# A path that fetches the last tile of a group row by row on the SyncE queue, beside the GpSimd gathers of a graph network

## The chip, the cores and the metric

The kernel runs on one core of a Trainium2 chip. The metric is the device time of one execution in microseconds, as the median of a few runs; a profiled execution shows where the time lies. The core has five engines that work side by side, each with its own instruction queue: TensorE (PE, with its weight loads PEld), VectorE (DVE), ScalarE (ACT), GpSimd (POOL) and SyncE (SP), which only issues transfers. The transfers themselves are done by 16 DMA engines.

## The reference

The kernel computes one message-passing layer of a graph network with 12,500 nodes and 412,500 edges, sorted by receiver. Cut to what matters:

```
h   = relu(layernorm(x))                                  # 12500 x 64
msg = concat(h[src], h[dst], edge_attr)                   # 412500 x 160
m   = silu(msg @ W1 + b1) @ W2 + b2                       # 412500 x 64
a   = softmax(silu(msg @ Wa1 + ba1) @ Wa2 + ba2, axis=0)  # over all edges
agg = segment_sum(m * a, dst)                             # 12500 x 64
out = x + silu(concat(h, agg) @ Wu1 + bu1) @ Wu2 + bu2
```

## The kernel before

**Node stage.** The nodes are normalised and multiplied once by the sender part and once by the receiver part of the two first layers (W1 and Wa1 side by side, C = 128 columns). That gives two tables in memory with one row of 128 floats (512 bytes) for each node: `ts_d`, looked up by sender, and `tr_d`, looked up by receiver.

**Edge loop.** The edges are cut into tiles of P = 128, and K = 8 tiles make a group: 3224 tiles, NG = 403 groups. For each group `load(g)` does the following:

- GpSimd issues eight indirect gathers (L412), one for each tile. A gather takes 128 sender numbers from a column of `src_sb` and brings 128 rows of `ts_d` into `gs[:, j, :]`, one row for each partition. The pool `gather` has 8 buffers of one group each.
- Every fourth group, SP loads the edge features and the receiver numbers of four groups (`eo`, L421, and `db`, L424), and `registers` (L399) loads four window bases from `base_sb` into SP's registers.
- SP loads two windows of 32 rows of `tr_d` at the address in a register (L431) into one of three `wins` buffers. Since the edges are sorted, all receivers of a group lie near each other.
- DVE builds a one-hot matrix from the receivers (L435), and PE multiplies it, together with the edge features, with the window (L439). So `pe` holds the receiver part and the edge part for the 1024 edges.

`begin(g)` adds the gathered rows to it on DVE (L444) and takes tanh on ACT (L445). `end(g)` forms both silu results (L455, L461), the attention logit (L463, L466) and, every fourth group, a running maximum. `sum_up` weights the edges of an earlier group (L507), sums them by receiver on PE (L513), projects them (L524) and adds them into `sums` in on-chip memory (L534 to L538). A buffer of `gather` is free again when `end(g)` has read it, and the gather of group g + 8 then goes into it.

**Order.** `load` runs AHEAD = 2 groups before `begin`. The instructions of DVE, ACT and PE in the loop are held in program order by `pin`. The gathers and SP's transfers are not: a planner orders each queue when the program is built, with earlier program lines first among those that it takes to be ready. From group 16 to about group 112 the loop also carries, every second group, a piece of work on the nodes (`node_bias` and `node_rest`, the `hb` loads of L315 and L333 and the stores of L324 and L335 on SP).

**Node update.** After the loop each node's sum is scaled and run through the update layers, and the result is written out.

The lines around which all this turns:

```
for g in range(AHEAD):
    load(g)
...
for g in range(NG):
    ...
    begin(g)
    ...
    if g + AHEAD < NG:
        load(g + AHEAD)
    ...
    end(g)
```

Of the kernel before, what the change touches and what calls it, by code (L numbers as in the profile page):

```python
# [42 lines left out]
F32 = mybir.dt.float32  # L43
I32 = mybir.dt.int32
AF = mybir.ActivationFunctionType
ALU = mybir.AluOpType
AX = mybir.AxisListType
ENG = mybir.EngineType
# [3 lines left out]
P = 128  # L52
# [3 lines left out]
C = 2 * U  # L56
S1 = U + 1
K = 8
# [7 lines left out]
B = 4  # L66
NQ = 4
TABLES = 4
EPS = 1e-5
NEG = -3.0e38  # L70
BIG = 3.0e38
# [5 lines left out]
WHY = "a receiver's number; windows past the last node are padded"  # L77


@with_exitstack  # L80
def gnn_kernel(ctx: ExitStack, tc: tile.TileContext, n_edges, x, src, dst, dst_row, first, edge,
               weights, out):
    nc = tc.nc
    NB = x.shape[0] // P
    T = src.shape[1]
    NG = T // K
    NP = NB * P
# [6 lines left out]
    ts_d = dram.tile([NP, C], F32, name="ts_d")  # L94
# [12 lines left out]
    part, at = {}, 0  # L107
# [43 lines left out]
    with tc.tile_pool(name="node1", bufs=1) as node1, \  # L151
# [23 lines left out]
        pin = tc.keep_in_program_order  # L175
# [15 lines left out]
        eps = node1.tile([P, 1], F32, name="eps")  # L191
        nc.vector.memset(eps, EPS)
        pin(nc.scalar.activation(node1.tile([P, 1], F32, name="spare"), eps, AF.Sqrt))
# [90 lines left out]
        for c, nn in chunks:  # L284
            tr = node.tile([P, CB, C], F32, name="tr")[:, :nn, :]
            for b in range(0, nn, 4):
                n = min(4, nn - b)
                pn = node_ps.tile([P, 4, C], F32, name="pn", bufs=4)
                for i in range(0, n, 2):
# [7 lines left out]
        pin(nc.scalar.dma_start(hT_d, hT))  # L297

    one_pass(tc, n_edges, locals())
    again = nc.values_load(wrong[0:1, 0:1], min_val=0, max_val=1,  # L300
                           skip_runtime_bounds_check_because="it is the outcome of a comparison")
# [36 lines left out]
def one_pass(tc, n_edges, v):  # L338
    nc = tc.nc
    NB, T, NG, NP, CB = (v[k] for k in ("NB", "T", "NG", "NP", "CB"))  # L340
# [3 lines left out]
    ts_d, tr_d, bq_d, edge, dst_row = (v[k] for k in ("ts_d", "tr_d", "bq_d", "edge", "dst_row"))  # L344
# [8 lines left out]
    pin = tc.keep_in_program_order  # L353

    with ExitStack() as ctx:
# [16 lines left out]
        for w in wins:  # L372
            nc.vector.memset(w, 0.0)
            for r in range(2):
                rows = slice(WR + r * DE, WR + (r + 1) * DE)
                nc.vector.tensor_copy(w[rows, :, r, :], we[rows, None, :].to_broadcast([DE, 2, C]))
        with tc.tile_pool(name="work2", bufs=2) as work2, \
                tc.tile_pool(name="small", bufs=3) as small, \
                tc.tile_pool(name="pre_ps", bufs=AHEAD + 1, space=PSUM) as pre_ps, \
                tc.tile_pool(name="one_ps", bufs=1, space=PSUM) as one_ps:  # L380
            pes, gss, lgs, ps_, psums, sps, pps, ees, mts = ({} for _ in range(9))


            w2t_ps = one_ps.tile([P, 4, P], F32, name="mt")[:U, 0, :S1]
# [4 lines left out]
            nc.tensor.matmul(w2u_ps, w2t, wu1a, start=True, stop=True)  # L389
            nc.vector.tensor_copy(w2u, w2u_ps)  # L390
            at_sp, at_dve = {}, {}


            tr_w = bass.AP(tensor=tr_d.tensor, offset=tr_d.offset,
# [2 lines left out]
            def registers(g, engine, at):  # L397
                n = min(NQ, NG - g)
                _, regs = nc.values_load_multi_w_load_instructions(  # L399
                    base_sb[0:1, g:g + n], engines=[engine], min_val=0, max_val=NP - 1,  # L400
                    skip_runtime_bounds_check_because=WHY)
                for i in range(n):
                    at[g + i] = regs[i]

            def load(g):

                t = g * K
                if g % NQ == 0:
                    registers(g, ENG.SP, at_sp)
                gs = gss[g] = gather.tile([P, K, C], F32, name="gs")  # L410
                for j in range(K):
                    nc.gpsimd.indirect_dma_start(  # L412
                        out=gs[:, j, :], out_offset=None, in_=ts_d[:, :],
                        in_offset=bass.IndirectOffsetOnAxis(ap=src_sb[:, t + j:t + j + 1], axis=0))
                if g % NQ == 0:
                    n = min(NQ, NG - g) * E2
                    eo = work2.tile([P, NQ, E2], F32, name="eo")
                    db = work2.tile([WR, NQ, E2], I32, name="db")
                    for i in range(g, min(g + NQ, NG)):
                        ees[i] = eo[:, i - g, :], db[:, i - g, :]  # L420
                    nc.sync.dma_start(eo.rearrange("p g e -> p (g e)")[WR:, :n],  # L421
                                      edge[:, g * E2:g * E2 + n])
                    for r in range(2):
                        nc.sync.dma_start(  # L424
                            db.rearrange("p g e -> p (g e)")[r * R:(r + 1) * R, :n],
                            bass.AP(tensor=dst_row.tensor, offset=dst_row[r:r + 1, g * E2:].offset,
                                    ap=[[0, R], [1, n]]))
                eo, db = ees.pop(g)
                win = wins[g % WINS]
                for r in range(2):  # L430
                    nc.sync.dma_start(win[r * R:(r + 1) * R, :, r, :],  # L431
                                      tr_w[bass.ds(at_sp[g], R), :, :])
                for h in range(2):
                    e = slice(h * E2 // 2, (h + 1) * E2 // 2)
                    pin(nc.vector.tensor_scalar(eo[:WR, e], db[:, e], bj[:, g, h:h + 1], None,  # L435
                                                op0=ALU.is_equal))
                pe = pes[g] = pre_ps.tile([P, K, C], F32, name="pe")
                for q in range(H):
                    pin(nc.tensor.matmul(pe[:, 2 * q:2 * q + 2, :], eo[:, q * P:(q + 1) * P],  # L439
                                         win[:, q // 2, :, :], start=True, stop=True))  # L440

            def begin(g):

                pin(nc.vector.tensor_tensor(gss[g], pes[g], gss[g], ALU.add))  # L444
                pin(nc.scalar.activation(pes[g], gss[g], AF.Tanh))  # L445

            def end(g):
# [94 lines left out]
            at, weighed = [None, None], [0]  # L542
# [28 lines left out]
            for g in range(AHEAD):  # L571
                load(g)
            done = 0
            for g in range(NG):
# [3 lines left out]
                if more and g == NG - 1:  # L578
                    next(more)
                begin(g)  # L580
                if more and g < NG - 1:
                    next(more)
# [6 lines left out]
                if g + AHEAD < NG:  # L589
                    load(g + AHEAD)  # L590
# [36 lines left out]
        with tc.tile_pool(name="upd1", bufs=1) as upd1, \  # L627
# [14 lines left out]
            for c in range(0, NB, 2 * H):  # L642
                n = min(H, (NB - c) // 2)
# [32 lines left out]
def general(tc, n_edges, v, dst):  # L676
# [7 lines left out]
    with ExitStack() as ctx:  # L684
        keep = ctx.enter_context(tc.tile_pool(name="keep_g", bufs=1))
        act_d = dram.tile([P, T, S1], F32, name="act_d")
        sum_d = [dram.tile([NP + P, S1], F32, name=f"sum_d{r}") for r in range(TABLES)]
        before = keep.tile([P, P], F32, name="before")
# [15 lines left out]
        rows = (NP + P) // P  # L704
        for r in range(TABLES):
            flat = sum_d[r].rearrange("(p b) f -> p (b f)", p=P)
# [63 lines left out]
        with tc.tile_pool(name="sums_g", bufs=2) as work, \  # L770
                tc.tile_pool(name="sums_g_ps", bufs=2, space=PSUM) as sums_ps:
            for g in range(0, T, G):
# [3 lines left out]
                for k in range(0, ng, K):  # L776
# [26 lines left out]
                    for j in range(K):  # L803
                        nc.gpsimd.indirect_dma_start(
                            out=sum_d[(t + j) % TABLES][:, :],
                            out_offset=bass.IndirectOffsetOnAxis(ap=to[:, j:j + 1], axis=0),
# [6 lines left out]
        with tc.tile_pool(name="upd_g", bufs=2) as work, \  # L813
                tc.tile_pool(name="upd_g_ps", bufs=2, space=PSUM) as upd_ps:
            for c in range(0, NB, CB):
                part = work.tile([P, TABLES, CB, S1], F32, name="part")
                for r in range(TABLES):
                    nc.sync.dma_start(part[:, r], sum_v[r][:, c:c + CB, :])
                for r in range(1, TABLES):
                    nc.vector.tensor_tensor(part[:, 0], part[:, 0], part[:, r], ALU.add)  # L820
# [95 lines left out]
```

## Time and profile before

| | us |
|---|---|
| median of 3 runs | 4156.85 (4156.84 to 4158.81) |
| the profiled execution | 4156.93 |
| its span, first to last instruction | 4155.2 |
| POOL busy | 3048.2 (73%) |
| DVE busy | 2874.9 (69%) |
| PE busy / PE weight loads | 2243.6 (54%) / 1682.4 (40%) |
| ACT busy | 599.4 (14%) |
| first gather starts / last gather starts | 52.0 / 4082.0 |

Busy time counts the work of an engine. Loading registers, waiting on semaphores and issuing transfers on SP are not counted as busy; their durations can still be read by line, under the name "SPq". A group of the page reads: line, engine, operation, output and inputs, shapes, count, then busy us and mean ns of one, then the idle time in front of it and what ended that. "issue" means that nothing in the profile was being waited for.

### The profile page before, as it was taken

The page shows a single profiled execution, that of the slowest core. Times are in us where ns is not written, and L with a number is a line of the kernel's source. Part 1 is how long each engine was busy: PE and PEld are TensorE (multiplying, and loading weights), DVE is VectorE, ACT ScalarE, POOL GpSimd, SP SyncE. Part 2 cuts the span into 40 slices and gives each one's busy share as a digit, 9 for nine tenths or more (in the row PEclk, how much of TensorE's full clock was granted, in tenths as well). Part 3 has the DMA queues.
Part 4 walks back from the last instruction along what each step waited for, and adds up shares of the span by engine and source line. Part 5 has one row for each costly group of instructions (what it writes and reads, how often), then busy time and mean ns, then how long its engine had stood idle before and what let it go on. Part 6 is the DMA issues. An engine that isn't in the chain of part 4 may idle for free.

```text
span 4155.2 us, 43768 instructions
## 1 busy us (share of the span) xinstructions
PE 2243.6 (54%) x10980; PEld 1682.4 (40%) x10980; DVE 2874.9 (69%) x7698; ACT 599.4 (14%) x1230; POOL 3048.2 (73%) x3236
## 2 busy tenths in 40 slices
PE   5545555545465555555555555555555555555555
PEld 4433333433344344434443344434433443444444
DVE  6767776666677676666766666666676666766668
ACT  3211111111111111111111111111111111111112
POOL 3777777777777777777777777777777777777772
PEclk8666666676666665665566656566566556656565
DMA  7433443433433333333333333333333333333323
GB/s 275 109 87 94 102 101 95 103 96 99 102 85 90 90 80 90 86 83 90 81 90 85 85 90 80 90 85 85 90 80 90 85 85 90 80 90 85 86 77 111
DMA packets 230872, 392.46 MB, mean 94 GB/s; under 512 B 97746, under 2 KB 156371, under 8 KB 217427
## 3 DMA queue, kind: packets, MB, share of 16 engines
q0 software_dynamic: 103168, 211.49, 20.6%
q1 hardware_dynamic: 126066, 168.42, 15.6%
q10 hardware_dynamic: 1376, 9.67, 0.6%
q8 instruction: 91, 1.49, 0.1%
q14 instruction: 171, 1.39, 0.1%
HBM read 363.56 MB, written 25.72 MB: 94 GB/s over the span
## 4 chain that ended last, share of the span: by engine, by line


## 5 line engine op out<-in xcount | busy, mean ns | idle before, releaser
L412 POOL DMA_INDIRECT gs<-ts_d,src_sb x3224 | 3046.6, 945 | 1033.9 <-issue 933.7
L439 PE MATMUL pe<-wins,eo 128*128 128x256 f32 x3224 | 1401.8, 611 | 1187.4 <-issue 1124.1
L439 PEld LDWEIGHTS pe<-wins,eo 128*128 128x128 f32 x3224 | 958.4, 312 | 1464.9 <-issue 1191.1
L444 DVE TENSOR_TENSOR gs<-pe,gs 128x1024 f32<-128x1024 f32 x403 | 491.7, 1220 | 1107.0 <-DMA gs<-ts_d,src_sb 1088.1
L445 ACT ACTIVATE pe<-gs 128x1024 f32<-128x1024 f32 x403 | 415.7, 1031 | 2751.9 <-DVE gs L444 2058.6
L507 DVE TENSOR_SCALAR wt<-iota_w,dloc,p 128x40 f32<-128x40 f32 x3224 | 723.1, 317 | 0.1
L513 PE MATMUL sp<-wt,acts 128*65 128x40 f32 x6448 | 585.3, 261 | 0.9 <-DVE wt L507 0.9
L513 PEld LDWEIGHTS sp<-wt,acts 128*65 128x65 f32 x6448 | 534.6, 173 | 26.7 <-DVE wt L507 1.0
L483 PE MATMUL mt<-ident,mx 128*128 128x128 f32 x103 | 48.4, 470 | 506.9 <-DVE sums L537 503.6
L455 DVE SCALAR_TENSOR_TENSOR acts<-pe,gs 128x512 f32<-128x512 f32 x403 | 271.7, 674 | 29.7 <-ACT pe L445 29.6
L463 DVE TENSOR_TENSOR pe<-pe,w_all 128x512 f32<-128x512 f32 x403 | 281.5, 699 | 12.8
L461 DVE SCALAR_TENSOR_TENSOR pe<-pe,gs 128x512 f32<-128x512 f32 x403 | 280.6, 696 | 11.2
L466 DVE TENSOR_REDUCE lg<-pe 128x8 f32<-128x512 f32 x403 | 277.0, 687 | 10.3
L435 DVE TENSOR_SCALAR eo<-db,bj 64x256 f32<-64x256 int32 x806 | 273.1, 376 | 7.6
L524 PEld LDWEIGHTS mt<-ss,w2u 65*64 65x64 f32 x806 | 99.8, 176 | 397.2 <-issue 383.8
L524 PE MATMUL mt<-ss,w2u 65*64 65x40 f32 x806 | 150.6, 281 | 166.1 <-DVE gm L490 148.8
L483 PEld LDWEIGHTS mt<-ident,mx 128*128 128x128 f32 x103 | 18.6, 181 | 519.9 <-DVE sums L537 515.7
L494 ACT ACTIVATE scale<-fall 128x1 f32<-128x1 f32 x103 | 20.9, 203 | 514.2 <-DVE fall L493 514.2
L538 DVE COPY sums<-nmax 64x40 f32 x403 | 78.2, 194 | 9.2 <-issue 0.3
L519 ACT COPY ss<-sp 65x40 f32<-65x40 f32 x403 | 73.5, 182 | 28.5 <-PE sp L513 28.3
L537 DVE TENSOR_TENSOR sums<-sums,mt 64x40 f32 x300 | 53.5, 178 | 3.3 <-PE mt L524 2.5
L320 ACT COPY bu<-mt 64x512 f32<-64x512 f32 x24 | 25.8, 1077 | 150.6 <-PE mt L317 150.6
(89 smaller groups left out, 592.0 us busy)
## 6 DMA issues: line engine op xcount, KB each, us to landing
gs<-ts_d,src_sb POOLq DMA_INDIRECT x3224
eo<-in_edge_dram SPq DMA_DIRECT2D x100, 512.0 KB
db<-in_dst_row_dram SPq DMA_DIRECT2D x200, 256.0 KB
wins<-tr_d SPq DMA_DIRECT2D x806, 32.0 KB
ts_d<-ts SPq DMA_DIRECT2D x5, 896.0 KB
tr_d<-tr ACTq DMA_DIRECT2D x5, 896.0 KB
hT_d<-hT ACTq DMA_DIRECT2D x1, 3136.0 KB
hb<-in_x_dram SPq DMA_DIRECT2D x24, 128.0 KB
```

The costliest lines, as they stand in the source:

```text
L412: nc.gpsimd.indirect_dma_start(out=gs[:, j, :], out_offset=None, in_=ts_d[:, :], in_offset=bass.IndirectOffsetOnAxis(ap=src_sb[:, t + j:t ...
L435: pin(nc.vector.tensor_scalar(eo[:WR, e], db[:, e], bj[:, g, h:h + 1], None, op0=ALU.is_equal))
L439: pin(nc.tensor.matmul(pe[:, 2 * q:2 * q + 2, :], eo[:, q * P:(q + 1) * P], win[:, q // 2, :, :], start=True, stop=True))
L444: pin(nc.vector.tensor_tensor(gss[g], pes[g], gss[g], ALU.add))
L445: pin(nc.scalar.activation(pes[g], gss[g], AF.Tanh))
L455: pin(nc.vector.scalar_tensor_tensor(acts[g % ACTS][:, :, 0:U], th[:, :, U:C], 1.0, gs[:, :, U:C], op0=ALU.add, op1=ALU.mult))
L461: pin(nc.vector.scalar_tensor_tensor(att, th[:, :, 0:U], 1.0, gs[:, :, 0:U], op0=ALU.add, op1=ALU.mult))
L463: pin(nc.vector.tensor_tensor(att, att, wa2[:, None, :].to_broadcast([P, K, U]), ALU.mult))
L466: pin(nc.vector.tensor_reduce(lgs[s][:, k:k + K], att, AX.X, ALU.add))
L507: pin(nc.vector.tensor_scalar(wt[:, j, :], iota_w[:, j // H, :], dloc[:, g * K + j:g * K + j + 1], p[:, k + j:k + j + 1], op0=ALU.is_equal ...
L513: pin(nc.tensor.matmul(sp, acts[g % ACTS][:, j, :], wt[:, j, :], start=j == 0, stop=j == K - 1))
L524: pin(nc.tensor.matmul(pp, w2u, sps.pop(g), start=True, stop=True))
```

## The change

A second way to fetch the last tile of a group is added. A tile so fetched does not come by an indirect gather on GpSimd but by 128 transfers of one row each on SP, whose addresses are registers that are loaded from a row of sender numbers.

- The sender numbers are given to the kernel a second time, as one row `src_row`.
- `rows_ahead(g)` loads the 128 numbers of group g's last tile into a tile of one partition and puts it into `rows_at[g]`. It is called with 11 at the start, and, when g % 11 is 5, with g + 11 // 2 + 11.
- `rows(g)` is called once in each `load(g)`, after the windows. When g is a multiple of 11, it looks for `g + 11` in `rows_at`, and if it is there, it takes a new tile `one_gs` for that group and notes it in `rows_to` and `alone`. For a group noted in `rows_to` it loads 12 sender numbers into registers and issues 12 row transfers, those of the numbers from 12 x (g % 11) on, up to 128.
- In `load`, a group that stands in `alone` has its gathers for seven tiles only. In `begin`, the add for such a group is made in two instructions, one of seven tiles and one of the tile that came alone.

```diff
+EVERY = 11
+ROWS = 12
+LOADS = 12
...
+            rows_at, rows_to = {}, {}
+
+            def rows_ahead(g):
+                if g < NG - 4:
+                    t = g * K + K - 1
+                    rows_at[g] = small.tile([1, P], I32, name="one_src", bufs=2)
+                    nc.sync.dma_start(rows_at[g], v["src_row"][:, t * P:(t + 1) * P])
+
+            def rows(g):
+                if g == 0:
+                    rows_ahead(EVERY)
+                if g % EVERY == 0:
+                    rows_at.pop(g, None)
+                    rows_to.clear()
+                    if g + EVERY in rows_at:
+                        rows_to[g + EVERY] = one = work2.tile([P, C], F32, name="one_gs")
+                        alone[g + EVERY] = one
+                if g % EVERY == EVERY // 2:
+                    rows_ahead(g + EVERY // 2 + EVERY)
+                for at, to in rows_to.items():
+                    i = g % EVERY * ROWS
+                    for a in range(i, min(i + ROWS, P), LOADS):
+                        n = min(LOADS, P - a)
+                        _, regs = nc.values_load_multi_w_load_instructions(
+                            rows_at[at][0:1, a:a + n], engines=[ENG.SP], min_val=0, max_val=NP - 1,
+                            skip_runtime_bounds_check_because=WHY)
+                        for k in range(n):
+                            nc.sync.dma_start(to[a + k:a + k + 1, :], ts_d[bass.ds(regs[k], 1), :])
...
                 gs = gss[g] = gather.tile([P, K, C], F32, name="gs")
-                for j in range(K):
+                for j in range(K - (g in alone)):
...
                                       tr_w[bass.ds(at_sp[g], R), :, :])
+                rows(g)
...
-                pin(nc.vector.tensor_tensor(gss[g], pes[g], gss[g], ALU.add))
+                n = K - (g in alone)
+                pin(nc.vector.tensor_tensor(gss[g][:, :n, :], pes[g][:, :n, :], gss[g][:, :n, :], ALU.add))
+                if n < K:
+                    pin(nc.vector.tensor_tensor(gss[g][:, n, :], pes[g][:, n, :], alone.pop(g), ALU.add))
...
+        "src_row": padded(src, t * P)[None],
```

More of the change, by code (lines that the diff above doesn't have):

```diff
@@ L80, in gnn_kernel @@
 @with_exitstack
-def gnn_kernel(ctx: ExitStack, tc: tile.TileContext, n_edges, x, src, dst, dst_row, first, edge,
+def gnn_kernel(ctx: ExitStack, tc: tile.TileContext, n_edges, x, src, src_row, dst, dst_row, first, edge,
                weights, out):
@@ L380, in one_pass @@
                 tc.tile_pool(name="one_ps", bufs=1, space=PSUM) as one_ps:
-            pes, gss, lgs, ps_, psums, sps, pps, ees, mts = ({} for _ in range(9))
+            pes, gss, lgs, ps_, psums, sps, pps, ees, mts, alone = ({} for _ in range(10))
             w2t_ps = one_ps.tile([P, 4, P], F32, name="mt")[:U, 0, :S1]
```

## The prediction

> **What bounds the kernel now.** I read the page's groups of instructions first, then a table of windows over the steady loop, then the start of the timeline, because the change puts work on SP's queue and the start is where that queue has least room. The groups, each with count, busy us and mean ns, then idle time before it:
>
> ```profile
> L412 POOL DMA_INDIRECT gs<-ts_d,src_sb x3224 | 3046.6, 945 | 1033.9 <-issue 933.7
> ...
> L444 DVE TENSOR_TENSOR gs<-pe,gs 128x1024 f32<-128x1024 f32 x403 | 491.7, 1220 | 1107.0 <-DMA gs<-ts_d,src_sb 1088.1
> ```
>
> The reader should see a queue that never rests: 3224 gathers of 945 ns, and before them idle time put down to "issue", which is no wait for anybody. DVE, the next busiest, loses 1107.0 us in front of the add of L444, nearly all of it to the landing of gathers: it waits for POOL, not POOL for it. The windows view (length, busy us and count of PE, PEld, DVE, ACT, POOL; clock, DMA share, GB/s) gives the pace:
>
> ```profile
> 2000.00:3000.00 1000.00, 544.93 (x2629) 410.18 (x2628) 685.39 (x1853) 127.18 (x275) 755.89 (x802) 0.61 0.35 86
> ```
>
> 802 gathers in 1000 us are 1.247 us each; the timeline of POOL shows 0.94 us of work and 0.30 us of gap at a fixed step of 1.249. From the first start (52.0) to the last (4082.0) there are 3223 steps, 4030.0/3223 = 1.250, so POOL sets the time from 52 to 4083 us. The last 72 us are the node update, which comes after it.
>
> **The Trainium skill.** "DMA: Bandwidth & Descriptors", section "Issuing engines are not separate DMA queues", says that whichever engine issues a transfer, the same 16 DMA engines run it, and that another issuer saves only sequencer time. Here sequencer time on POOL is what bounds the loop, and the DMA engines have room (share 0.35 above), so the trace agrees that moving a gather could pay. The same page, "Latency and other measured facts", puts a register load from memory at about 600 ns at least; the trace has 298 ns for four registers, so the measured value decides and the page only serves as a middle value for twelve. Its section "Anatomy of one DMA" gives about 2 us from issue to completion; the trace has SP waiting 1.5 to 1.7 us for such a landing (L315 for xb_d).
>
> **The change, part by part.** First what the code will really do. `alone` gets an entry only where `g + EVERY in rows_at`, for g = 0, 11, 22, ... So rows_at must hold 11, 22, 33. It is filled by `rows_ahead(11)` at g = 0, and afterwards at g % 11 == 5 with the key g + 11 // 2 + 11 = g + 16. For g = 5, 16, 27 that is 21, 32, 43, ... up to 395. With an even EVERY, half and half make a whole; with 11, 5 + 5 is 10, and every later key is one short of a multiple of 11. The test finds 11 at g = 0 and never anything again. Hence one group of 403, group 11, loses its eighth gather. Its 128 rows are issued in groups 0 to 10 (ten times 12 and once 8, 11 register loads), and 35 of the 36 index loads bring numbers that nobody uses. What follows is:
>
> *POOL:* one gather fewer, 1 x 1.249 = -1.25 us on the path.
>
> *SP, rows.* The nearest instructions are the window loads, also one register address each, and the register load of base_sb (instructions by source and by tile; min/median/max ns):
>
> ```profile
> L431 SPq FUSED_REGOPS  x806: 37/37/51, 80.6 to 4041.2; - x162
> L431 SPq MOVE wins<-tr_d x806: 29/29/140, 86.3 to 4041.3; - x162
> L431 SPq DMA_DIRECT2D wins<-tr_d x806: 316/317/513, 86.3 to 4041.4; - x162
> ...
> L399 SPq TENSOR_LOAD <-base_sb x101: 294/298/1556, 79.0 to 4013.4; - x101
> L167 SPq DMA_DIRECT2D base_sb<-in_first_dram x1: 306/306/306, 8.6 to 8.6; - x1
> ```
>
> 37 + 29 + 317 = 383 ns; two windows in a row take 0.82 us, so 0.40 a row. Base_sb, a load into one partition, issues in 306 ns, so one row is not dearer than a window. A load of 12 registers lies between 0.3 us (all fixed) and 0.9 us (in proportion); I take 0.6. Sum: 128 x 0.40 + 11 x 0.6 = 57.8 us of SP in all, about 5.4 us in each of eleven groups. Each of those groups has 0.8 us of windows and about 1.0 us of other loads on SP (per four groups 1.5 us for edges and receivers, 2.5 us for the node stage), together 7.2 us against POOL's 8 x 1.249 = 10.0. On the path: nothing, if SP's lateness stays within the cover below.
>
> *SP, index loads:* 36 x 0.31 = 11 us over the whole loop, and at most 36 x 1.7 = 61 us if each makes SP wait for a landing. SP spends 1885.9 us merely waiting for PE at L431, so this is hidden. Steadily, a window for group g + 3 goes out when PE is done with group g, 30 us before it is wanted.
>
> *DVE:* in group 11 one add of 1220 ns becomes one of 128x896 (1092 ns at L206) and one of 128x128 (0.29 us at L658): +0.16 us once. DVE waits 293.6 us in 100 groups in front of that add, 2.9 us a group, and this hides it; bare, it would cost 0.16.
>
> *The DMA engines:* 128 rows of 512 bytes are 64 KB beside 392 MB. Bound for a slower gather: zero, since POOL's step stays 1.249 while the 1 MB of edge and receiver loads go out.
>
> *The start,* where cover could run out. From the timeline (start, length, idle before):
>
> ```profile
> 77.58 1.38 SPq L421 DMA_DIRECT2D eo<-in_edge_dram  x1
> ...
> 86.33 3.29 SPq L431 DMA_DIRECT2D wins<-tr_d  x6
> ...
> 98.95 1.22 DVE L444 TENSOR_TENSOR gs<-pe,gs 128x1024 f32<-128x1024 f32 x1 [8.07 <-PE pe L439]
> ...
> 103.32 0.70 DVE L461 SCALAR_TENSOR_TENSOR pe<-pe,gs 128x512 f32<-128x512 f32 x1
> ...
> 134.13 0.94 POOL L412 DMA_INDIRECT gs<-ts_d,src_sb  x1 [0.30 <-issue]
> ```
>
> The gather pool has eight buffers, so gather 65, the first of group 8, needs group 0's buffer. It starts at 52.0 + 64 x 1.249 + 2.1 (three longer gaps at 85 to 93 us) = 134.1, the last row. Its last reader in group 0 (L461) ended at 104.0. So the consumers of group 0 may be 30 us later before POOL feels it. Later groups run at 7 us until they catch up with POOL at 10 us, so this cover grows by about 3 us a group. In program order rows(0) and rows(1) stand between the first windows and those of groups 1 and 2: 5 to 11 us late, plus the landing of the index row, perhaps 10 us while the DMA share is 1.0 (up to 95 us). Also, SP makes some issues wait for older landings they share no data with:
>
> ```profile
> SPq L166 <- DMA w_all<-in_weights_dram: 0.9, 1, 0.9
> ```
>
> Altogether 10 to 25 us late, under 30. Cost taken: 0. Bounds: no gain is to be had here, since POOL does not wait for the start; the loss is worked out below.
>
> *Sum against the profiled execution:* 4156.93 - 1.25 + 0 = 4155.68. Its span is 4155.2 with 1.7 us around it, which stays; the median of the runs, 4156.85, lies 0.08 from it. Prediction 4155.7 us, 0.03% down, which no measurement here resolves: I take 0.2% (8.3 us) as the least change that can be told from none.
>
> **Rivals.** *A, the change does what its words say.* If all of groups 11, 22, ..., 396 lost a gather, 36 x 1.249 = 45.0 us would go and the time be 4111.9. For it: the saturated POOL above, and that SP could carry 7.2 us a group. Against: the keys, 21 and not 22. I give 3 in 100, for a misreading of mine.
>
> *B, SP's queue delays the start: slower.* The order on SP is not that of the program: the second edge load, wanted from group 4, stands at 77.58 ahead of the first windows, and hb loads of the node stage, due after group 16, stand at 103.4. If all 128 rows were pulled ahead of the first windows, SP would be busy 57.8 us from 79, of which some 7 us are free (it waits till 86.3 for wins to be cleared). The first windows come 50 us late, group 0's buffer is free at 154 and not 104, and POOL stands still 50 - 30 = 20 us: 4155.7 + 20 = 4175.7. It decides from a delay of 39.6 us, where the stall is 1.25 + 8.3 = 9.6 us: about 103 rows ahead of the first windows. Against it: after one early edge load the queue did turn to the windows, though receiver loads for the same groups (at 89.67) and hb loads were still to come, so earlier work of the program seems to go first once it can. 9 in 100.
>
> *C, a smaller stall at the start.* Rows ahead of the windows in part, with slow landings while the DMA share is near 1, a delay of 30 to 39 us: 4156 to 4165, still no change. 7 in 100.
>
> **How the numbers follow.** Likeliest, 81 in 100: 4155.7, between 4153.5 and 4159 from the spread of the runs (4156.84 to 4158.81) around it. With C the middle reaches to about 4161; A and B stay outside with 12 in 100. Range 4153 to 4161. Faster by over 0.2%: A, 0.03. Slower by over 0.2%: B, 0.09. Within: 0.88.
>
> **What would show it.** POOL's gathers x3223 in place of x3224, at 945 ns and a step of 1.249; if it is x3188, A is right. L444 with 402 adds of 128x1024, one of 128x896, one of 128x128. On SP 128 row loads, 11 register loads of a new line and 36 index loads of src_row. First gather at 52, gather 65 near 134; a POOL gap of many us there, with the first wins later than 125, would be B. The last gather near 4081, with the same 72 us behind it. It would be wrong if the keys do match, if SP's order puts a hundred rows first, or if a later burst on SP held windows back by more than their 30 us and the 60 us that eight buffers give behind it.

## The result, and the profile after

The changed kernel takes 4154.34 us (median, 4153.86 to 4156.06), the kernel before 4156.89 us beside it (4155.9 to 4158.85). The ratio is 0.9994, 95% interval 0.9986 to 1.0001: no difference that this measurement resolves. The prediction was 4155.7 us, no change.

The profiled execution took 4156.06 us with a span of 4154.3 (before: 4156.93 and 4155.2). Its groups of instructions, of which the first answers to L412 before and the second to L444 before:

```profile
L444 POOL DMA_INDIRECT gs<-ts_d,src_sb x3223 | 3045.4, 945 | 1033.4 <-issue 933.2
...
L478 DVE TENSOR_TENSOR gs<-pe,gs 128x1024 f32<-128x1024 f32 x403 | 491.7, 1220 | 1083.6 <-DMA gs<-ts_d,src_sb 1071.4
...
L468 DVE TENSOR_SCALAR eo<-db,bj 64x256 f32<-64x256 int32 x806 | 279.3, 384 | 31.2 <-DMA db<-in_dst_row_dram 23.5
```

The last of these rows was, before:

```profile
L435 DVE TENSOR_SCALAR eo<-db,bj 64x256 f32<-64x256 int32 x806 | 273.1, 376 | 7.6
```

One gather is gone, not 36, and each of the others costs the same 945 ns. DVE waits for gathers as before, 1071.4 us in place of 1088.1. New in the last row is that DVE waited 23.5 us for receiver numbers (`db`). The windows view of the steady loop can hardly be told from that of before:

```profile
2000.00:3000.00 1000.00, 542.57 (x2629) 407.60 (x2627) 687.41 (x1852) 127.19 (x275) 756.08 (x801) 0.61 0.34 86
```

By source line and tile (minimum, median and maximum ns, then first and last start), the gathers, the new work of SP, and the add of the tile that came alone:

```profile
L444 POOL DMA_INDIRECT gs<-ts_d,src_sb x3223: 938/944/1192, 51.8 to 4080.2; - x190
...
L423 SPq DMA_DIRECT2D one_gs<-ts_d x128: 224/228/293, 92.2 to 173.7; - x128
...
L402 SPq DMA_DIRECT2D one_src<-in_src_row_dram x36: 217/287/1448, 78.5 to 485.8; - x36
...
L419 SPq TENSOR_LOAD <-one_src x11: 712/936/1005, 91.2 to 169.8; - x11
...
L480 DVE TENSOR_TENSOR gs<-pe,one_gs x1: 270/270/270, 194.1 to 194.1; 128x128 f32<-128x128 f32 x1
```

The 128 rows went out once, between 92 and 174 us, for one group. The 36 index loads were all issued by 485.8 us, though the program has them spread over all 403 groups: the planner pulled them forward. The register load of 12 takes 0.94 us. The start on SP's timeline (start, length, count):

```profile
78.52 1.45 SPq L402 DMA_DIRECT2D one_src<-in_src_row_dram  x1
...
87.26 0.90 SPq L463 DMA_DIRECT2D wins<-tr_d  x2
92.17 5.28 SPq L423 DMA_DIRECT2D one_gs<-ts_d  x12
97.71 0.87 SPq L463 DMA_DIRECT2D wins<-tr_d  x2
99.76 4.83 SPq L423 DMA_DIRECT2D one_gs<-ts_d  x12
...
119.20 0.79 SPq L456 DMA_DIRECT2D db<-in_dst_row_dram  x2
```

and on DVE's (in brackets the idle time before it and what ended it):

```profile
103.09 0.70 DVE L497 SCALAR_TENSOR_TENSOR pe<-pe,gs 128x512 f32<-128x512 f32 x1
...
105.17 1.21 DVE L478 TENSOR_TENSOR gs<-pe,gs 128x1024 f32<-128x1024 f32 x1
...
111.13 1.23 DVE L478 TENSOR_TENSOR gs<-pe,gs 128x1024 f32<-128x1024 f32 x1 [0.78 <-PE pe L472]
123.61 0.61 DVE L468 TENSOR_SCALAR eo<-db,bj 64x256 f32<-64x256 int32 x2 [11.25 <-DMA db<-in_dst_row_dram]
...
158.60 0.73 DVE L468 TENSOR_SCALAR eo<-db,bj 64x256 f32<-64x256 int32 x2 [12.25 <-DMA db<-in_dst_row_dram]
```

In the kernel before, the adds of groups 1 and 2 stood here:

```profile
107.08 1.21 DVE L444 TENSOR_TENSOR gs<-pe,gs 128x1024 f32<-128x1024 f32 x1
...
112.19 1.21 DVE L444 TENSOR_TENSOR gs<-pe,gs 128x1024 f32<-128x1024 f32 x1
```

The windows of group 0 go out first, then twelve rows, then the windows of group 1: the order of the program, not the pile-up of rival B. Group 0's last reader (L497) ends at 103.8, as before (104.0), and the adds of groups 1 and 2 are no later than before. The next receiver numbers stand behind rows on SP, and DVE waits 11 and 12 us for them. Neither wait reaches POOL: gather 65 starts with the usual gap of 0.30, and in the whole trace no gap between gathers after 94 us is longer than 0.35:

```profile
134.08 1.04 POOL L444 DMA_INDIRECT gs<-ts_d,src_sb  x1 [0.30 <-issue]
```

### The profile page after: what moved, and what is told of

The parts are those of the page before. It is cut to its first block, busy times and chain, and to the rows that moved or that the text cites. A ratio compares the mean times of both kernels' runs of the same rounds, so it can differ in the third digit from the quotient of the medians.

```text
span 4154.3 us, 44195 instructions
## 1 busy us (share of the span) xinstructions
PE 2246.1 (54%) x10980; PEld 1683.3 (41%) x10980; DVE 2882.5 (69%) x7699; ACT 599.3 (14%) x1230; POOL 3046.9 (73%) x3235
## 4 chain that ended last, share of the span: by engine, by line
## 5 line engine op out<-in xcount | busy, mean ns | idle before, releaser
L444 POOL DMA_INDIRECT gs<-ts_d,src_sb x3223 | 3045.4, 945 | 1033.4 <-issue 933.2
L472 PE MATMUL pe<-wins,eo 128*128 128x256 f32 x3224 | 1402.7, 611 | 1189.5 <-issue 1091.7
L472 PEld LDWEIGHTS pe<-wins,eo 128*128 128x128 f32 x3224 | 957.9, 311 | 1468.2 <-issue 1184.2
L478 DVE TENSOR_TENSOR gs<-pe,gs 128x1024 f32<-128x1024 f32 x403 | 491.7, 1220 | 1083.6 <-DMA gs<-ts_d,src_sb 1071.4
L468 DVE TENSOR_SCALAR eo<-db,bj 64x256 f32<-64x256 int32 x806 | 279.3, 384 | 31.2 <-DMA db<-in_dst_row_dram 23.5
L497 DVE SCALAR_TENSOR_TENSOR pe<-pe,gs 128x512 f32<-128x512 f32 x403 | 280.6, 696 | 11.2
L560 PEld LDWEIGHTS mt<-ss,w2u 65*64 65x64 f32 x806 | 99.2, 175 | 394.2 <-issue 381.3
L560 PE MATMUL mt<-ss,w2u 65*64 65x40 f32 x806 | 149.9, 280 | 162.8 <-DVE gm L526 146.0
L530 ACT ACTIVATE scale<-fall 128x1 f32<-128x1 f32 x103 | 20.9, 203 | 521.9 <-DVE fall L529 521.9
```

Of the source, the lines that this page charges most:

```text
L444: nc.gpsimd.indirect_dma_start(out=gs[:, j, :], out_offset=None, in_=ts_d[:, :], in_offset=bass.IndirectOffsetOnAxis(ap=src_sb[:, t + j:t ...
L478: pin(nc.vector.tensor_tensor(gss[g][:, :n, :], pes[g][:, :n, :], gss[g][:, :n, :], ALU.add))
L497: pin(nc.vector.scalar_tensor_tensor(att, th[:, :, 0:U], 1.0, gs[:, :, 0:U], op0=ALU.add, op1=ALU.mult))
L560: pin(nc.tensor.matmul(pp, w2u, sps.pop(g), start=True, stop=True))
```

## Experiments

### First series: the change as it was meant, other doses, and all rows at once

In this series the kernel before itself took 5457 to 5472 us (median 5464.16) and not 4157; why is not known, so the ratios of this series say nothing about the result above. They are given because they show what the same edits do where POOL does not set the time (shown below for the mended key). None of the gains that were expected came.

The mended key, so that 36 groups give up a gather:

```diff
-                    rows_ahead(g + EVERY // 2 + EVERY)
+                    rows_ahead(g + EVERY - EVERY // 2 + EVERY)
```

> The key is mended (g + 11 - 5 + 11), so groups 11, 22, ..., 396 each lose one gather, 36 in all. Theory (the wrong key is what kept the change small, POOL sets the time): 36 x 1.249 = 45.0 us less than before, about 4112, gathers x3188. Rival (SP's queue cannot carry rows all the way: in the changed kernel DVE waited 11 and 12 us for receiver loads standing behind rows): the gain is mostly lost, 4140 or more, with DVE waiting for db in the steady loop.

Every 22nd group, six rows per group (18 groups give up a gather; an even EVERY needs no mending):

```diff
-EVERY = 11
-ROWS = 12
-LOADS = 12
+EVERY = 22
+ROWS = 6
+LOADS = 6
```

> EVERY = 22 with 6 rows and one register load of 6 a group; 22 is even in the sense that 11 + 11 makes 22, so the keys match and groups 22, 44, ..., 396 would be served, but 22 // 2 = 11 and the call at g = 11 asks for g + 33 = 44, so every later group is found; 18 gathers fewer. Theory: 18 x 1.249 = 22.5 us less, about 4134.4. Rival (a fixed gain that is not from the gathers): as the changed kernel, about 4154.

Every 8th group, sixteen rows per group (49 groups):

```diff
-EVERY = 11
-ROWS = 12
-LOADS = 12
+EVERY = 8
+ROWS = 16
+LOADS = 16
```

> EVERY = 8 with 16 rows and one register load of 16 a group: 4 + 4 = 8, so the keys match and groups 8, 16, ..., 392 lose a gather, 49 in all. SP per group: 16 x 0.40 + about 1.2 for the register load + 0.9 windows + 0.4 other loads = 8.9 us. Theory (SP below POOL's 9.8 us is hidden): 49 x 1.249 = 61.2 us less, about 4095.7. Rival (SP is as good as full): no better than with EVERY = 11 mended, above 4112.

The keys of the change, but all 128 rows of group 11 issued in `load(0)`, ahead of its windows (rival B built on purpose):

```diff
-ROWS = 12
+ROWS = 128
...
+                rows(g)
                 win = wins[g % WINS]
...
-                rows(g)
```

> The changed kernel with all 128 rows of group 11 in load(0), ahead of its windows in the program (ROWS = 128, rows(g) called before the windows); still one gather fewer. Theory (the start has a cover of 30 us, beyond which POOL stands still): 128 x 0.40 + 11 x 0.94 = 61.5 us of SP from about 80, first windows near 142 instead of 87, group 0's buffer free near 159 instead of 104, POOL idle some 25 us before gather 65, time about 4180. Rival (the start does not reach the end, the consumers catch up whatever happens): as the changed kernel, about 4154.5.

And the mended key once more:

> The kernel with the mended key once more, on whatever chip comes, since the kernel before took 5464 us in the runs beside the first one and not 4157. Theory (where the kernel before takes 4157, POOL sets the time and SP is hidden): 45.0 us less than the kernel before beside it, about 4112, and SP about 8 us busy per group of 9.9. Rival (SP's longer stream of instructions is itself the loss, on any chip): slower by several hundred us here too.

| kernel | us | ratio, 95% interval |
|---|---|---|
| mended key, 12 rows a group | 6185.6 | 1.1311, 1.1279 to 1.1343 |
| every 22nd, 6 rows a group | 5578.92 | 1.0201, 1.0183 to 1.0218 |
| every 8th, 16 rows a group | 7039.07 | 1.2864, 1.2842 to 1.2885 |
| 128 rows at once | 5534.32 | 1.0125, 1.0110 to 1.0140 |
| mended key, once more | 6164.03 (before: 5458.22) | |

The more rows each group carries, the slower, though each step takes gathers away. In the kernel with the mended key, POOL's group:

```profile
L444 POOL DMA_INDIRECT gs<-ts_d,src_sb x3188 | 3016.5, 946 | 3037.7 <-issue 2984.4
```

SP's wait at the windows for L472, PE's product with a window (us in all, times, longest), here and in the changed kernel of the section above:

```profile
SPq L463 <- PE pe L472: 15.2, 10, 6.8
...
SPq L463 <- PE pe L472: 1806.8, 257, 15.0
```

SP's timeline here, and one register instruction of each row here and in the same kernel in the second series (minimum, median and maximum ns):

```profile
2000.88 12.68 SPq L423 DMA_DIRECT2D one_gs<-ts_d  x6
...
2019.36 7.53 SPq L423 DMA_DIRECT2D one_gs<-ts_d  x12
```

```profile
L423 SPq MOVE one_gs<-ts_d x4608: 1/29/1396, 144.7 to 6034.0; - x192
...
L423 SPq MOVE one_gs<-ts_d x4608: 29/29/42, 89.2 to 3933.9; - x192
```

POOL, with gathers of the usual length, is idle for 3037.7 us; it does not set the time here. SP waits 15.2 us for L472 in place of 1806.8: it has hardly any time left, and sets the pace. Its rows cost from 0.6 us each (7.53/12) to 2.1 (12.68/6), not 0.40. From first to last gather this kernel takes 6003.6 us, 14.9 a group. The trace shows how SP is slowed: some 2800 of its 17,900 instructions, of whatever kind, begin 0.70 or 1.40 us after the one before, 2.6 ms in all, and in the second series' trace of the same kernel ten do. Of PE's instructions eight do here and 18 there, so PE is not slowed in this way. What causes them stays open, and so does whether they slow the kernel before, of which there is no trace in this series.

### Second series: the same questions where the kernel before takes its usual time

The changed kernel again, the mended key, and the burst, beside a kernel before of 4161 to 4163 us.

> The changed kernel itself beside the kernel before. Theory (one gather of 3224 is gone and the rest is hidden): within 0.2% of the kernel before, 1.25 us below it where POOL sets the time. Rival (the 128 rows and 36 index loads on SP cost something where SP is slow, as in the runs where the kernel before takes 5460 us): slower by up to 1%, as in the run with all rows at the start.

> The kernel with the mended key (36 groups lose a gather) beside a kernel before that, it is hoped, takes about 4160 us. Theory (POOL sets the time, SP's rows are hidden in 8 of its 10 us a group): 36 x 1.249 = 45.0 us less, about 4115. Rival (SP carries too much and its lateness reaches POOL, as where the kernel before takes 5460 us): above 4150, with waits of DVE and PE for db, wins or rows in the steady loop.

> All 128 rows of group 11 in load(0), ahead of its windows, beside a kernel before of about 4160 us. Theory (cover of 30 us at the start): first windows near 142 instead of 87, group 0's buffer free near 159, POOL idle some 25 us before gather 65, in all some 24 us more than before, about 4185. Rival (the consumers catch up and the start does not reach the end): as the changed kernel, about 4158.

| kernel | us | ratio, 95% interval |
|---|---|---|
| the changed kernel | 4158.22 (4156.04 to 4160.62) | 0.9993, 0.9984 to 1.0002 |
| mended key | 4121.14 (4115.77 to 4123.3) | 0.9902, 0.9885 to 0.9918 |
| 128 rows at once, ahead of the windows | 4192.56 (4192.29 to 4193.46) | 1.0072, 1.0055 to 1.0089 |

**The mended key** is 41.6 us faster than the kernel before (4162.72 beside it). Its gathers, the windows view, and SP's waits (L560 is PE's projection) and timeline:

```profile
L444 POOL DMA_INDIRECT gs<-ts_d,src_sb x3188: 940/944/1191, 50.5 to 4039.4; - x200
```

```profile
2000.00:3000.00 1000.00, 562.50 (x2649) 422.39 (x2649) 691.76 (x1873) 128.33 (x277) 756.36 (x800) 0.61 0.37 88
```

```profile
SPq L463 <- PE mt L560: 324.9, 182, 8.3
SPq L463 <- PE pe L472: 303.2, 77, 10.3
```

```profile
2013.83 0.86 SPq L463 DMA_DIRECT2D wins<-tr_d  x2
2015.86 4.82 SPq L423 DMA_DIRECT2D one_gs<-ts_d  x12
2021.51 0.86 SPq L463 DMA_DIRECT2D wins<-tr_d  x2
```

36 gathers fewer, and POOL as full as before: 800 in 1000 us. From 50.5 to 4039.4 there are 3988.9 us, 41.1 less than the 4030.0 of before. A step is 3988.9/3187 = 1.2516 us where it was 1.2504, which over the loop is the missing 4 us of the 45.0. The changed kernel has a step of 1.2509 in this series, though (4030.6/3222), so nearly half of that belongs to the series. No gap between gathers after 92 us is longer than 0.35, so POOL never stood still for SP. The DMA engines' share is 0.37 in place of 0.35; that the added rows stretch the gathers is likely, but not shown. SP takes 7.7 us for this group (2013.83 to 2021.51), which has no other loads. On the mean of the groups after the node work it is about 7.8: both waits together are 628 us, nearly all in those 300 groups, 2.1 each, and POOL's pace is 9.9. The prediction's budget had 7.2. In the 100 groups with node work SP has almost nothing left: its waits for PE at the windows are under 7 us between 200 and 1200 us. The wait for L472 fell from 1806.8 us in the changed kernel to 303.2: the cover is being used up.

**The burst** is 29.8 us slower. On SP's, DVE's and POOL's timelines:

```profile
89.59 64.23 SPq L423 DMA_DIRECT2D one_gs<-ts_d  x128
154.70 3.34 SPq L464 DMA_DIRECT2D wins<-tr_d  x6
```

```profile
160.71 1.23 DVE L478 TENSOR_TENSOR gs<-pe,gs 128x1024 f32<-128x1024 f32 x1 [70.48 <-PE pe L472]
...
165.08 0.70 DVE L497 SCALAR_TENSOR_TENSOR pe<-pe,gs 128x512 f32<-128x512 f32 x1
```

```profile
166.54 0.94 POOL L444 DMA_INDIRECT gs<-ts_d,src_sb  x1 [33.95 <-issue]
```

The first windows go out at 154.7, 67.4 us later than in the changed kernel, and group 0's last reader (L497) ends at 165.8, 62.0 us later than there (103.8). The gather that needs group 0's buffer, the 65th, waits 33.95 us where the gap is 0.30 otherwise: 33.7 us lost. So 62.0 - 33.7 = 28 us of the buffer's lateness were covered; the prediction had 30. The time follows: against the kernel before beside each, the burst loses 29.8 us and the changed kernel gains 2.9, 32.8 apart. Rival B's mechanism is real; only the order on SP, which kept rows behind windows, keeps the changed kernel from it.

### Third series: how much SP can carry, and the index loads that nobody uses

Every 8th group with 16 rows again, and every 6th with 22:

```diff
-EVERY = 11
-ROWS = 12
-LOADS = 12
+EVERY = 6
+ROWS = 22
+LOADS = 11
```

The changed kernel without its later index loads:

```diff
-                if g % EVERY == EVERY // 2:
-                    rows_ahead(g + EVERY // 2 + EVERY)
```

> EVERY = 8, ROWS = LOADS = 16: the keys g + 4 + 8 at g % 8 == 4 are multiples of 8, so 49 groups give up a gather. Theory (POOL's queue sets the time while SP's work per group stays under POOL's step): POOL gives up 49 x 1.249 = 61.2 us. SP carries per group 16 rows x 0.40 = 6.4, a register load of 16 at about 0.94 x 16/12 = 1.25, windows 0.86 and about 1.0 of other loads, 9.5 us in all against POOL's 9.84: just under, so about 61 us below the kernel before, ratio about 0.985, with SP's waits for PE at the windows nearly gone. Rival: with the waits for landings, which cost 1.4 us each in the kernel with the mended key, SP passes POOL in the groups with node work (12 us there), and the gain is smaller than the 41.6 us of the mended key, or becomes a loss: ratio 0.990 to 1.02.

> EVERY = 6, ROWS = 22, LOADS = 11: 66 groups give up a gather, which by POOL alone would be 66 x 1.249 = 82.4 us less, ratio 0.980 (rival: SP's work stays hidden). Theory: SP is overfilled and becomes the bound. Per group 22 rows x 0.40 = 8.8, two register loads of 11 at 0.86 = 1.7, windows 0.86, about 1.0 of other loads: 12.4 us against POOL's 9.78. Over 403 groups 403 x 12.4 = 4997 us in place of 4030: about 950 us slower, ratio about 1.23, at least 1.15. POOL would then show long gaps before the first gather of a group, waiting for a buffer.

> The changed kernel without the later calls of rows_ahead: the 35 index loads that nobody uses are gone, the rows of group 11 stay. Theory: those loads are hidden behind POOL, so the time is that of the changed kernel, ratio to the kernel before 0.9990 to 1.0000. Rival: they cost their issue or a landing each, 11 to 61 us, and the ratio falls to 0.985 to 0.997.

| kernel (before: 4156.57) | us | ratio, 95% interval |
|---|---|---|
| every 8th, 16 rows a group | 4406.11 (4402.31 to 4408.34) | 1.0602, 1.0585 to 1.0620 |
| every 6th, 22 rows a group | 6412.74 (6411.36 to 6413.55) | 1.5429, 1.5403 to 1.5455 |
| changed kernel, one index load | 4153.15 (4151.55 to 4155.46) | 0.9991, 0.9983 to 1.0000 |

**Without the later index loads** the ratio is the changed kernel's within the intervals (0.9991 and 0.9994), so they are hidden, as the prediction had it.

**Every 8th group** loses where 61 us of gain were expected; the rival's reading holds, though it put the loss at 2% at most and 6% were measured. Its waits of SP and DVE, and SP's timeline:

```profile
SPq L463 <- PE pe L472: 32.9, 18, 8.1
```

```profile
DVE eo L468 <- DMA db<-in_dst_row_dram: 903.0, 94, 18.7
```

```profile
3005.96 0.87 SPq L463 DMA_DIRECT2D wins<-tr_d  x2
...
3014.95 0.86 SPq L463 DMA_DIRECT2D wins<-tr_d  x2
...
3026.49 0.87 SPq L463 DMA_DIRECT2D wins<-tr_d  x2
3028.58 8.51 SPq L423 DMA_DIRECT2D one_gs<-ts_d  x16
3037.34 0.86 SPq L463 DMA_DIRECT2D wins<-tr_d  x2
...
3046.67 0.88 SPq L463 DMA_DIRECT2D wins<-tr_d  x2
```

SP hardly waits for PE any more, and DVE not for gathers (4.6 us in all) but for the receiver numbers that SP brings: SP is the bound. Four groups take SP 9.0, 11.5, 10.9 and 9.3 us, 10.2 on the mean, against the 9.84 that POOL needs for 7.88 gathers. The expected sum of 9.5 left out the landings (arrivals of earlier transfers) that SP stops for: in the third of these groups the 16 rows took 8.51 us and not 6.47, and the queue's waits there are 2.0 us for `db`. That is 2.0 of the 2.7 us by which the four groups exceed the sum. Where the node work adds to it (600 to 1000 us) POOL gets 261 gathers in 400 us (before: 321), 12.1 us a group. The loss comes mostly from there, for between 2000 and 3000 us it still gets 783 (before: 802).

**Every 6th group** has SP as the bound as expected (its waits for L472 are 20.9 us in all), but at 15.5 us a group ((6289.3 - 50.6)/403) and not 12.4. Two consecutive register loads of 11 in it, each by itself:

```profile
L419 SPq TENSOR_LOAD <-one_src x1: 2526/2526/2526, 2010.6 to 2010.6; - x1
...
L419 SPq TENSOR_LOAD <-one_src x1: 1340/1340/1340, 2018.9 to 2018.9; - x1
```

The expectation had 0.86 us for each. Twelve such loads make the fill of one group's tile. Their medians over all fills, in order, with the byte at which each begins in the row of numbers:

```
byte      0    44    88   132   176   220   264   308   352   396   440   484 (7 numbers)
us     1.25  2.53  2.46  2.53  1.24  2.53  2.52  2.53  1.24  2.53  2.46  1.73
```

The cheap ones begin at multiples of 16 bytes. A fill of 12 loads costs 25.5 us, 4.3 a group, in place of 1.7: 2.6 of the 3.1 us by which the sum fell short.

### The offset of the register load by itself

This kernel is the one with the mended key and makes the same number of register loads; but here the stretches of 12 rows begin 0, 1, 2 or 3 numbers earlier in turn. Against that kernel:

```diff
-                    i = g % EVERY * ROWS
-                    for a in range(i, min(i + ROWS, P), LOADS):
-                        n = min(LOADS, P - a)
+                    i = g % EVERY * ROWS - at // EVERY % 4
+                    for a in range(max(i, 0), min(i + ROWS, P), LOADS):
+                        n = min(i + ROWS, P) - a
```

> The kernel with the mended key, but the eleven stretches of 12 rows of a group begin 0, 1, 2 or 3 numbers earlier in turn from one such group to the next, so that the register loads of 12 stand at 0, 12, 8 or 4 bytes past a multiple of 16. Nothing else changes: 128 rows, 11 register loads, 36 groups. Theory (the offset sets the price of a register load): loads in the unshifted fills stay at 0.93 us, those in the shifted fills take about 2.5 us each, as the loads of 11 at such offsets did in the EVERY = 6 kernel, so SP's work per group grows by about 1.6 us in three groups of four, 1.2 us on the mean. In the plain part of the loop, where SP waits some 600 us for PE in all at the windows, that is hidden (7.7 + 1.6 = 9.3 against 9.87). In the 100 groups with node work SP has almost no wait at the windows left (2.7 us between 200 and 1200 us), so there it comes on the path: up to 120 us, the time between 4121 and 4240 beside a kernel before of 4157 to 4161, more likely above the kernel before than below. Rival (the count sets the price, 11 being an awkward number, not the offset): loads of 12 stay at 0.93 us wherever they stand, and the time stays at that of the mended key, about 4119 to 4123, ratio 0.990.

It takes 4124.37 us (4122.63 to 4128.13), ratio 0.9921, 0.9905 to 0.9938. All register loads, and then those of one shifted and of one unshifted fill:

```profile
L419 SPq TENSOR_LOAD <-one_src x396: 708/2490/3108, 88.9 to 3940.8; - x198
...
L419 SPq TENSOR_LOAD <-one_src x11: 935/2653/2722, 2002.5 to 2105.6; - x11
...
L419 SPq TENSOR_LOAD <-one_src x11: 714/937/1158, 2113.5 to 2210.6; - x11
```

Over the 36 fills the loads of 12 in the middle of a fill have these medians: at a multiple of 16 bytes 0.94 us, at 4, 8 or 12 bytes past one 2.66 us in each case. So the offset sets the price, and the rival (the count alone) falls. What was expected of the time falls too: 27 fills with some 17 us more on SP should have shown, in the 100 groups with node work, up to 120 us. It is 8.5 us by the medians, each kernel against the kernel before beside it (33.1 us gained and not 41.6), and 9.5 by the spans of the traced executions (4123.5 and 4114.0). Between 200 and 1200 us SP's wait in front of L327 (a store of the node work) fell from 75.7 to 17.9 us and that for `db` from 36.5 to 9.1, so 85 of these us lay in waits that had room in them. The expectation had counted only SP's waits at the windows as room. POOL missed 7 gathers between 1000 and 1400 us (313 against 320), 8.7 us, and none elsewhere.

## Why the prediction was right, step by step

- **The keys** (21, 32, 43, never a multiple of 11). Right: x3223, one group with a separate add (L480 x1), 128 rows, 11 register loads, 36 index loads. Mending that one expression gave x3188 and 41.6 us, against 45.0 by rival A's working. So what the words of the change promised is missing because of the key.
- **POOL bounds, 1.249 us a gather.** Right in size for 36 gathers (41.1 of 45.0 from first to last gather). For the one gather, -1.25 us lies inside every interval; the medians showed -2.55 and -2.9 for the changed kernel and -3.4 without its later index loads, the profiled executions -0.87. What of that goes beyond -1.25 is not resolved.
- **SP, rows.** 0.40 us a row: measured 4.83/12 = 0.40, though the transfer's own issue is 228 ns and not the 317 of a window. **The register load** was mis-sized: 0.94 us, above the 0.9 of the upper bound, where 0.6 was taken. SP's sum is 128 x 0.40 + about 11 x 0.94 = 61.5 us and not 57.8. Hidden all the same. "Latency and other measured facts" of the Trainium skill's "DMA: Bandwidth & Descriptors", which served for the middle value, gives a floor of about 600 ns and no slope; here 4 numbers take 0.298 us, below that floor, 8 take 0.71, 12 take 0.94 and 16 take 1.16, where they begin at a multiple of 16 bytes.
- **SP, index loads.** Right: hidden, shown by leaving 35 of them out. That they would spread over the loop was wrong; they were all issued by 486 us.
- **DVE.** The two adds took 1.07 + 0.27 = 1.34 us for the 1.22 of one: +0.12, where the prediction had 0.16.
- **The start.** The cover of 30 us was right (28 by the burst). The windows of groups 1 and 2 went out some 10 and 16 us late, as foreseen (97.7 and 104.8; before, all six window loads lie between 86.3 and 89.6), but no add came later for it. The landing of the index row, taken as perhaps 10 us, cost SP a wait of 2.7. What held DVE up was something the prediction had not named: the receiver numbers, which stood behind rows, for 11 and 12 us. It made no difference since it is far below the cover.
- **Rival B** was rightly kept as the way to a loss, and its place and price hold: predicted 20 us of stall for a buffer 50 us late, measured 33.7 for one 62.0 us late. It did not come about because the first windows went ahead of the rows.

## What to carry to other kernels

Before costing an edit, follow its keys and conditions through a few rounds of the loop by hand: the words of this change were worth 42 us, its code nothing that these runs resolve. Where work goes from a full queue to one that seems idle, sum the receiving queue's time per round, with its stops for landings, against the full queue's; here the gain had turned into a loss where they met (7.8 against 9.9 us gained 1%, 10.2 against 9.8 lost 6%). And waits of a queue are not all equal: a stop for a landing can be room as well as cost, which here only a run told.

## What the runs showed of the hardware that was not expected

- A load of 12 registers costs SP 0.94 us where the numbers begin at a multiple of 16 bytes and about 2.66 us where they don't. Eleven at a multiple of 16 bytes take 1.24, more than twelve.
- A transfer of one 512-byte row at a register's address occupies SP for 0.40 us, with the register work that goes with it: a third of the 1.249 us in which POOL gathers 128 such rows.
- In the first series the same kernel before took 5464 us. In the kernel with the mended key gathers kept their 945 ns there, while instructions of SP came only every 0.70 or 1.40 us, for 2.6 of 6.2 ms in all. There the edit that gains 1% elsewhere lost 13%. The cause is open.
